# The first MLP product of one and a half batches, between the attention units, by seven block products

## The chip, the cores and the metric

The kernel runs on one core of a Trainium2 chip. A core has engines that work side by side, each with a queue of its own that it takes strictly in order: TensorE (PE: matmuls, with its weight loads shown as PEld), VectorE (DVE), ScalarE (ACT), GpSimd (POOL) and SyncE (SP), which here only issues DMAs. Matmul results go to PSUM, everything else lies in SBUF. The metric is the device time of one execution in microseconds (us). A difference under 0.5% counts as none.

## What is computed

One cross-attention block with its MLP, in fp32, for B = 4 batches of 512 rows of x and 512 rows of context, D = 512, 16 heads of 32, an inner width of 2048. Cut to what matters:

```python
h = layer_norm(x, ln1_w, ln1_b)
q = h @ q_w + q_b;  k = ctx @ k_w + k_b;  v = ctx @ v_w + v_b       # 16 heads of 32
attn = softmax(where(mask, q @ k.T / sqrt(32), -max))
hidden = (attn @ v) @ cproj_w + cproj_b + x
y = layer_norm(hidden, ln2_w, ln2_b)
y = gelu_tanh(y @ fc_w + fc_b)                                      # 512 -> 2048, "fc"
out = hidden + y @ proj_w + proj_b                                  # 2048 -> 512, "proj"
```

## The kernel before

**Units.** The attention is cut into NW = 16 groups `w` (batch w // 4, four heads each) times four tiles of 128 query rows: 64 units, u = 4w + qt. A unit issues `scores` (L252): PE puts the scores of four heads into `sc`, the one score buffer of four PSUM banks, so the scores of the next unit wait until the four minimum operations on VectorE (L263, output `ptt` and `mn`, with the mask `mb`) have read it; ACT takes four exps (L267). Then `turn` (L271) transposes the exps on VectorE into `tb` (L282); in odd units it also takes the reciprocal of the sums (L287), copies it on ACT (`rr`, L289) and transposes the rest (L290, L291). After two units, `exchange` (L300) sends `tb` to `pT` by 16 DMAs (L325), which SP's queue issues one by one. There is one `pT` for most pairs of units: the next exchange is issued only once `attend` (L328) of the pair before has multiplied its result into `oT` (VectorE, L347). `attend` is the matmuls `av` (L342); "attend 26" in the prediction is that of the 26th pair. Where a pair takes place is set by AT and LAG.

**Work between units.** PE's other work is put between the units by lists written out by hand: `first[w]` and `later[w]`, of chains such as `prep_k`, `prep_q`, `prep_v`, `cproj` (`accc`), the transposes of a norm (`tp`), fc (`accf`) and proj (`accp`). Where an entry is a tuple, its four members belong to the four units; otherwise `run` (L725) shares the list among the units by its costs, CHAIN = 3.4 and TURN = 0.5. `some(n)` takes the next n pieces of the MLP list: all fc and proj of batch 0, then those of half of batch 1 (SPLIT = 1, FIRST = 2 quarters). LN2 of a batch is `stat2`, `ln_rs` (`rs`, on GpSimd), `norm2` (L147) and `ln2_turn`, which leaves `yT`. GpSimd adds biases to the residual rows (`c_bias`, `proj_bias`, L354) and to v (L249).

**fc before.** `fc(b, f)` (L445) is four matmuls of 128 x 128 by 128 x 512 into one PSUM bank and one gelu by ACT, straight from PSUM. exp and gelu need different tables in ACT, so each turn from one to the other is an ACT_TABLE_LOAD. Weights go through a ring of MW = 8 slots: `load_mlp` (L434) issues the next load on SP's queue when the work that used a slot is issued.

**The tail.** What is left after the last unit, half of batch 1 and all of batches 2 and 3, is done in `last_mlps` (L513) with seven products of blocks in place of eight (Strassen's scheme in Winograd's form): for a pair of f, `fc_pair` (L541) forms sums of weight blocks (`a_sums`), sums of `yT`'s blocks (`b_sums`, in `y_sums`), seven products of two matmuls 128 x 128 by 128 x 256 each into four half-banks (`q`), and four adds on VectorE (L531) that put the results together, a copy of one on ACT (`p1`, L564) and four gelus. `project` does the same for proj (q1p to q7p).

Of the kernel before, what the change touches and what calls it, by code (L numbers as in the profile page):

```python
# [52 lines left out]
def xattn_block(ctx: ExitStack, tc: tile.TileContext, x, encT, mask, q_w, k_w, v_w, c_w, fc_w, p_w, vecs, rows, out):  # L53
# [391 lines left out]
    def fc(b, f):  # L445
        q, k = divmod(f, FQ)
        acc = acc_tile(f"accf_{b}_{f}")
        for d in range(ND):
            nc.tensor.matmul(acc, S["fcw", b, f][:, d, :], S["yT", b][:, d, :], start=(d == 0), stop=(d == ND - 1))  # L449
        nc.scalar.activation(  # L450
            gT[q % 2][:, k, :], acc, AF.Gelu_apprx_tanh, bias=vec[:, FCB + f : FCB + f + 1], scale=1.0
        )
# [22 lines left out]


    NP = NF // 2
    HL = L // 2

    def sub(o, x0, x1):  # L480
        nc.vector.tensor_tensor(o, x0, x1, ALU.subtract)  # L481

    def a_sums(a11, a12, a21, a22, s1, s2, s3, s4):
        nc.vector.tensor_tensor(s1, a21, a22, ALU.add)
        sub(s3, a11, a21)
        sub(s2, s1, a11)
        sub(s4, a12, s2)

    def b_sums(b11, b12, b21, b22, t1, t2, t3, t4):
        sub(t1, b12, b11)  # L490
        sub(t2, b22, t1)
        sub(t3, b22, b12)
        sub(t4, b21, t2)
# [19 lines left out]
    def last_mlps():  # L513
        last, ring = pools(ctx, last=1, ring=2)
        ps_last = ctx.enter_context(tc.tile_pool(name="ps_last", bufs=4, space=PSUM))
        ys = last.tile([P, 4, 2, HL], F32, tag="ys", name="ys")
# [10 lines left out]
        def acc_half(name):  # L527
            return acc_tile(name).rearrange("p (i l) -> p i l", i=2)

        def add(engine, o, x0, x1):  # L530
            engine.tensor_tensor(o, x0, x1, ALU.add)  # L531

        def y_blocks(b):
            return [S["yT", b][:, 2 * k : 2 * k + 2, j * HL : (j + 1) * HL] for k in range(2) for j in range(2)]

# [5 lines left out]
        def fc_pair(b, c, first, sums):  # L541
            a11, a12, a21, a22 = (wa[c % 2][:, i, 2 * k : 2 * k + 2] for i in range(2) for k in range(2))
            y11, y12, y21, y22 = y_blocks(b)
            s1, s2, s3, s4 = (ws[c % 2][:, i] for i in range(4))
# [4 lines left out]
            uc, u34, h = (ring.tile([P, 2, HL], F32, tag=n, name=f"{n}_{b}_{c}") for n in ("uc", "u34", "h"))

            def product(o, a, y):
                for k in range(2):
                    nc.tensor.matmul(o, a[:, k], y[:, k], start=(k == 0), stop=(k == 1))  # L553
# [391 lines left out]
```

## Time and profile before

| | us |
|---|---|
| median of 3 executions | 810.03 |
| lowest and highest | 807.67, 810.45 |
| profiled execution | 810.09 |
| its span, first to last instruction | 808.3 |
| PE busy, share | 791.9, 98% |
| DVE busy, share | 553.6, 68% |
| ACT busy, share | 360.8, 45% |
| POOL busy, share | 98.0, 12% |
| the tail's products begin at | 558.7 |

How to read the lines: a group's line has the source line, engine, operation, outputs and inputs by the program's names, shapes and the number of instructions; after the first bar the busy time and the mean time of one in nanoseconds; after the second the idle time of the engine just before them and what ended it. A timeline's line has the start, the duration, the engine, the line and the operation; idle time of the engine before it stands in brackets with its releaser. The chain of work goes back from the last instruction to what released each step; its lines have start, duration, what. A table by windows gives the stretch, its length, the busy time of PE, PEld, DVE, ACT and POOL with instructions in brackets, the share of full TensorE clock granted, the DMA share and GB/s.

### The profile page before, as it was taken

To read this page: it belongs to the slowest core of one execution; us is meant where nothing else is said; L and a number is where in the kernel's file an instruction comes from. 1 tells how busy PE (TensorE), PEld (TensorE's weight loads), DVE (VectorE), ACT (ScalarE), POOL (GpSimd) and SP (SyncE) were. 2 spreads that over 40 slices of the span, in tenths; PEclk is the share of its full clock that TensorE was granted. 3 is DMA by queue.
4 is the path that set the end of the run, shared out by engine and by line. 5 is a ranking of instruction groups with operands and counts; after the bars stand their busy time and mean duration, and the time that the engine had idled before them with its cause. 6 is when DMAs were issued, how large, how long until landed. Compare 5 with 4: busy or idle time off the path is not lost.

```text
span 808.3 us, 11790 instructions
## 1 busy us (share of the span) xinstructions
PE 791.9 (98%) x4082; PEld 481.2 (60%) x4082; DVE 553.6 (68%) x1145; ACT 360.8 (45%) x785; POOL 98.0 (12%) x112
## 2 busy tenths in 40 slices
PE   9999999979999999999999999999999999999998
PEld 6545455544454544535554333446888888888887
DVE  3788998876678665877778997636738993368511
ACT  2666755638673646556643469600312330023200
POOL 1110030030000030001131000120050021200011
PEclk9999999989999999999999999999999999999999
DMA  9889989837797877778768799883335330023001
GB/s 329 287 222 244 241 219 265 225 96 185 185 245 176 223 201 191 176 197 201 177 140 218 196 259 226 216 252 117 108 100 181 107 117 14 27 79 92 1 14 39
DMA packets 60955, 137.13 MB, mean 170 GB/s; under 512 B 12464, under 2 KB 15664, under 8 KB 60768
## 3 DMA queue, kind: packets, MB, share of 16 engines
q1 hardware_dynamic: 59472, 132.43, 61.2%
q0 software_dynamic: 896, 2.82, 1.1%
q10 hardware_dynamic: 528, 1.14, 0.7%
q8 instruction: 32, 0.52, 0.3%
q14 instruction: 27, 0.22, 0.1%
HBM read 58.22 MB, written 6.82 MB: 80 GB/s over the span
## 4 chain that ended last, share of the span: by engine, by line
PE 80%; DVE 7%; SPq 7%; DMA 3%; issue 1%; POOL 0%; ACT 0%; DVEq 0%; POOLq 0%
PE q L553 15%; PE accf L449 9%; PE accp L459 8%; PE accc L383 7%; SPq L325 7%; PE av L342 6%; PE sc L259 6%; PE acck L215 4%; PE accq L225 4%; PE accv L237 4%; DVE ptt L263 3%; PE q5p L593 2%; PE q3p L593 2%; PE q7p L593 2%; PE q6p L593 2%; PE q1p L593 2%
## 5 line engine op out<-in xcount | busy, mean ns | idle before, releaser
L267 ACT ACTIVATE ptt<-ptt,mn 128x512 f32<-128x512 f32 x256 | 182.2, 713 | 142.8 <-DVE mn L263 142.6
L263 DVE CUSTOM_DVE_ANT_0 ptt<-sc,mb 128x512 f32<-128x512 f32 x256 | 161.1, 685 | 45.6 <-PE sc L259 45.5
L282 DVE STREAM_TRANSPOSE tb<-ptt 128x1024 f32<-128x1024 f32 x96 | 119.1, 1242 | 10.4 <-ACT ptt L267 8.0
L449 PE MATMUL accf<-yT,pbt 128*128 128x512 f32 x192 | 87.3, 601 | 0.0
L459 PE MATMUL accp<-pbt,gt 128*128 128x512 f32 x192 | 86.5, 600 | 0.0
L259 PE MATMUL sc<-pbt 32*128 32x512 f32 x512 | 73.1, 640 | 4.8 <-DVE mn L263 2.6
L553 PE MATMUL q<-ys,gt 128*128 128x256 f32 x320 | 75.1, 379 | 0.0
L553 PEld LDWEIGHTS q<-ys,gt 128*128 128x128 f32 x320 | 60.8, 190 | 8.3
L449 PEld LDWEIGHTS accf<-yT,pbt 128*128 128x128 f32 x192 | 35.0, 190 | 50.2 <-issue 45.4
L459 PEld LDWEIGHTS accp<-pbt,gt 128*128 128x128 f32 x192 | 35.2, 190 | 48.8 <-issue 45.8
L237 PEld LDWEIGHTS accv<-ptt,xe 128*128 128x128 f32 x512 | 58.9, 192 | 8.2 <-issue 5.4
L237 PE MATMUL accv<-ptt,xe 128*128 128x128 f32 x512 | 60.5, 276 | 0.0
L215 PE MATMUL acck<-xe,ptt 128*128 128x512 f32 x128 | 59.0, 603 | 0.0
L553 PE MATMUL q<-yT,gt 128*128 128x256 f32 x240 | 58.1, 379 | 0.5 <-DVE gt L481 0.5
L225 PE MATMUL accq<-xe,ptt 128*128 128x512 f32 x128 | 58.4, 599 | 0.0
L383 PE MATMUL accc<-wc,oT 128*128 128x512 f32 x128 | 56.6, 596 | 0.0
L249 POOL TENSOR_TENSOR v<-v,row 128x512 f32<-128x512 f32 x16 | 20.4, 1274 | 278.5 <-ACT v L242 278.4
L557 ACT ACTIVATE ga<-uc,vec 128x256 f32<-128x256 f32 x40 | 20.4, 511 | 75.5 <-DVE uc L531 75.5
L553 PEld LDWEIGHTS q<-yT,gt 128*128 128x128 f32 x240 | 45.5, 190 | 7.4 <-DVE gt L481 0.9
L342 PE MATMUL av<-pT,v 128*32 128x256 f32 x768 | 48.1, 392 | 1.6 <-DMA pT<-tb 1.5
L267 ACT ACTIVATION_READ_ACCUMULATOR ptt<-ptt,mn 128x1 f32 x256 | 48.3, 189 | 0.0
L564 ACT COPY p<-q 128x256 f32<-128x256 f32 x20 | 7.1, 354 | 92.0 <-PE q L553 92.0
(121 smaller groups left out, 957.9 us busy)
## 6 DMA issues: line engine op xcount, KB each, us to landing
pT<-tb SPq DMA_DIRECT2D x384, 136.0 KB, 2.4
pbt<-p_w_dram SPq DMA_DIRECT2D x40, 256.0 KB, 3.1
gt<-fc_w_dram SPq DMA_DIRECT2D x40, 256.0 KB, 2.7
gt<-tb SPq DMA_DIRECT2D x64, 136.0 KB, 3.4
xe<-tb SPq DMA_DIRECT2D x56, 136.0 KB, 3.3
pbt<-fc_w_dram SPq DMA_DIRECT2D x24, 256.0 KB, 4.3
ptt<-k_w_dram SPq DMA_DIRECT2D x16, 256.0 KB, 3.9
xe<-encT_dram SPq DMA_DIRECT2D x16, 256.0 KB, 4.8
```

The source lines that it names most:

```text
L215: nc.tensor.matmul(acc, S["wk", w][:, d, :], eT[:, d, :], start=(d == 0), stop=(d == ND - 1))
L225: nc.tensor.matmul(acc, S["wq", w][:, d, :], xT[:, d, :], start=(d == 0), stop=(d == ND - 1))
L237: nc.tensor.matmul(acc[:, ts(t, P)], eT[:, d, ts(t, P)], S["wv", w][:, d, :], start=(d == 0), stop=(d == ND - 1),)
L259: nc.tensor.matmul(sc[:, h, :], qT[r, ts(qt, P)], kT[r, :], start=True, stop=True)
L263: nc.vector.tensor_tensor_reduce(out=s, in0=sc[:, h, :], in1=S["mb", w // NG], scale=1.0, scalar=FMAX, op0=ALU.add, op1=ALU.min, accum_out=mn,
L267: nc.scalar.activation(s, s, AF.Exp, bias=mn, scale=-1.0, accum_out=sums[:, qt, h : h + 1])
L282: nc.vector.transpose(*two_heads[k])
L342: nc.tensor.matmul(av[ts(h, HD), : 2 * P].rearrange(shape, **kw), v[:, t, ts(h, HD)], p[t][h], start=(t == 0), stop=(t == NT - 1),)
L383: nc.tensor.matmul(acc, S["oT", b][:, g, ts(t, P)], wc[:, g, :], start=(g == 0), stop=(g == NG - 1))
L449: nc.tensor.matmul(acc, S["fcw", b, f][:, d, :], S["yT", b][:, d, :], start=(d == 0), stop=(d == ND - 1))
L459: nc.tensor.matmul(acc, gT[q % 2][:, k, ts(t, P)], S["pw", b, q * FQ + k], start=(k == 0), stop=(k == FQ - 1))
L553: nc.tensor.matmul(o, a[:, k], y[:, k], start=(k == 0), stop=(k == 1))
```

## The change

The fc of batch 0 and of the first half of batch 1, done between the units, take the tail's scheme: `fc(b, c)` computes a pair of f by `fc_seven`, which the tail now calls too.

- Weights: three sums into `wsum` (two buffers) and one, s3, in place in the weight slot, by four adds of 128 x 256 on GpSimd for each pair; `fc_sums` issues them up to two pairs ahead, once the weights' loads have been issued.
- `yT`: three sums into `ys` and one, t3, in place in `yT`, four adds of 128 x 512 on VectorE for each batch (`y_sums`), in unit 21 for batch 0 and unit 47 for batch 1. For batch 1 they were at the start of the tail.
- Products: q1 and q26 lie in two `acc` banks, q57 and q34 in two more (in the tail: in two of its own half tiles); a copy of q1 on ACT (one buffer `p1`); four VectorE adds that write `gT` in place; then two gelus of 128 x 512 in place. In the tail the gelus were four of 128 x 256, each right after its add, and the first pair used s4 earlier.
- Order: a pair counts as two in `some(n)`; units with one fc now have a pair or none. Before, fc stood in units 22, 23, 25, 45, 58 (two each) and 26, 27, 31, 33, 36, 37, 42, 43, 57 and 59 to 63 (one each); now pairs stand in 22, 23, 25, 26, 33, 37, 42 and 45 (batch 0) and 57, 58, 60 and 62 (batch 1). Proj moves with it: some of batch 0's come later.
- `ys` and `wsum` are held from the start; the SBUF kept for GpSimd's DMA descriptors goes from its default to 4096 bytes.

```diff
@@ -87,6 +87,9 @@
     pb = pbt.rearrange("p (c i n) -> p c i n", c=NF // 2, i=2)
     pt = ptt.rearrange("p (s c n) -> p s c n", s=3, c=NF // 2)
 
+    ys = const.tile([P, 3, 2, L // 2], F32, tag="ys", name="ys")
+    wsum = const.tile([P, 2, 3, 2, P], F32, tag="wsum", name="wsum")
+
...
-    def fc(b, f):
-        q, k = divmod(f, FQ)
-        acc = acc_tile(f"accf_{b}_{f}")
-        for d in range(ND):
-            nc.tensor.matmul(acc, S["fcw", b, f][:, d, :], S["yT", b][:, d, :], start=(d == 0), stop=(d == ND - 1))
-        nc.scalar.activation(
-            gT[q % 2][:, k, :], acc, AF.Gelu_apprx_tanh, bias=vec[:, FCB + f : FCB + f + 1], scale=1.0
-        )
-        count[1] += 1
+    def a_sums(a11, a12, a21, a22, s1, s2, s3, s4, engine=None):
+        add(engine or nc.vector, s1, a21, a22)
+        sub(s3, a11, a21, engine)
+        sub(s2, s1, a11, engine)
+        sub(s4, a12, s2, engine)
+    def b_sums(b11, b12, b21, b22, t1, t2, t3, t4):
+        sub(t1, b12, b11)
+        sub(t2, b22, t1)
+        sub(t3, b22, b12)
+        sub(t4, b21, t2)
+    def y_blocks(b):
+        return [S["yT", b][:, 2 * k : 2 * k + 2, j * HL : (j + 1) * HL] for k in range(2) for j in range(2)]
+    def y_sums(b):
+        y = y_blocks(b)
+        b_sums(*y, ys[:, 0], ys[:, 1], y[1], ys[:, 2])
+    def fc_seven(b, c, g, a, s, half):
+        y11, t3, y21, y22 = y_blocks(b)
+        t1, t2, t4 = (ys[:, i] for i in range(3))
+        s1, s2, s3, s4 = s
+        q1, q26 = (acc_half(f"{n}_{b}_{c}") for n in ("q1", "q26"))
+        q57, q34 = (half(f"{n}_{b}_{c}") for n in ("q57", "q34"))
+        p1 = small.tile([P, HL], F32, tag="p1", bufs=1, name=f"p1_{b}_{c}")
+        g = g.rearrange("p i (j l) -> p (i j) l", j=2)
+        def product(o, x, y):
+            for k in range(2):
+                nc.tensor.matmul(o, x[:, k], y[:, k], start=(k == 0), stop=(k == 1))
+        product(q1[:, 0], a[0][:, 0:2], y11)
+        nc.scalar.copy(p1, q1[:, 0])
+        product(q26[:, 0], a[0][:, 2:4], y21)
+        product(q26[:, 1], s2, t2)
+        add(nc.vector, g[:, 0:4:3], q26, p1[:, None, :].broadcast_to([P, 2, HL]))
+        product(q57[:, 1], s3, t3)
+        product(q57[:, 0], s1, t1)
+        u2 = g[:, 3:4]
+        add(nc.vector, g[:, 1:3], q57, u2.broadcast_to([P, 2, HL]))
+        add(nc.vector, g[:, 3], q57[:, 0], g[:, 2])
+        product(q34[:, 0], s4, y22)
+        product(q34[:, 1], a[1][:, 2:4], t4)
+        add(nc.vector, g[:, 1:3], q34, g[:, 1:3])
+        for i in range(2):
+            f = 2 * c + i
+            h = g[:, 2 * i : 2 * i + 2]
+            nc.scalar.activation(h, h, AF.Gelu_apprx_tanh, bias=vec[:, FCB + f : FCB + f + 1], scale=1.0)
+    fc_pairs = [(b, q * FQ // 2 + i) for b in range(SPLIT + 1) for q in range(NQ if b < SPLIT else FIRST) for i in range(2)]
+    def raw_pair(b, c):
+        return [S["fcw", b, 2 * c + i] for i in range(2)]
+    def fc_sums():
+        while count[3] < len(fc_pairs) and count[3] < count[4] + 2:
+            b, c = fc_pairs[count[3]]
+            if ("fcw", b, 2 * c + 1) not in S:
+                return
+            x, y = raw_pair(b, c)
+            s = wsum[:, count[3] % 2]
+            a_sums(x[:, :2], x[:, 2:], y[:, :2], y[:, 2:], s[:, 0], s[:, 1], y[:, :2], s[:, 2], nc.gpsimd)
+            S["ws", b, c] = s[:, 0], s[:, 1], y[:, :2], s[:, 2]
+            count[3] += 1
+    def fc(b, c):
+        q, k = divmod(2 * c, FQ)
+        fc_seven(b, c, gT[q % 2][:, k : k + 2, :], raw_pair(b, c), S["ws", b, c], acc_half)
+        count[1] += 2
+        count[4] += 1
         load_mlp()
+        fc_sums()
 
...
-        def fc_pair(b, c, first, sums):
-            a11, a12, a21, a22 = (wa[c % 2][:, i, 2 * k : 2 * k + 2] for i in range(2) for k in range(2))
-            y11, y12, y21, y22 = y_blocks(b)
-            s1, s2, s3, s4 = (ws[c % 2][:, i] for i in range(4))
-            t1, t2, t3, t4 = (ys[:, i] for i in range(4))
-            q1, q62 = (acc_half(f"{n}_{b}_{c}") for n in ("q1", "q62"))
-            q75, q43 = (half_tile(f"{n}_{b}_{c}") for n in ("q75", "q43"))
-            p1 = ring.tile([P, HL], F32, tag="p1", name=f"p1_{b}_{c}")
-            uc, u34, h = (ring.tile([P, 2, HL], F32, tag=n, name=f"{n}_{b}_{c}") for n in ("uc", "u34", "h"))
-            def product(o, a, y):
-                for k in range(2):
-                    nc.tensor.matmul(o, a[:, k], y[:, k], start=(k == 0), stop=(k == 1))
-            def gelu(i, j, src):
-                f = 2 * c + i
-                nc.scalar.activation(
-                    ga[:, c, i, j * HL : (j + 1) * HL], src, AF.Gelu_apprx_tanh,
-                    bias=vec[:, FCB + f : FCB + f + 1], scale=1.0,
-                )
+        def fc_pair(b, c, sums):
             sums()
-            product(q1[:, 0], a11, y11)
-            nc.scalar.copy(p1, q1[:, 0])
-            product(q62[:, 1], a12, y21)
-            if first:
-                product(q43[:, 1], s4, y22)
-            product(q62[:, 0], s2, t2)
-            add(nc.vector, uc, q62, p1[:, None, :].broadcast_to([P, 2, HL]))
-            gelu(0, 0, uc[:, 1])
-            product(q75[:, 0], s3, t3)
-            product(q75[:, 1], s1, t1)
-            add(nc.vector, u34, q75, uc[:, :1].broadcast_to([P, 2, HL]))
-            add(nc.vector, uc[:, 0], q75[:, 1], u34[:, 0])
-            gelu(1, 1, uc[:, 0])
-            if not first:
-                product(q43[:, 1], s4, y22)
-            product(q43[:, 0], a22, t4)
-            add(nc.vector, h, q43, u34)
-            gelu(1, 0, h[:, 0])
-            gelu(0, 1, h[:, 1])
+            fc_seven(b, c, ga[:, c], [wa[c % 2][:, i] for i in range(2)],
+                     [ws[c % 2][:, i] for i in range(4)], half_tile)
...
-        y_sums(SPLIT)
...
-        return [(CHAIN, lambda f=f: fc(b, f)) for f in range(q * FQ, (q + 1) * FQ)]
+        return [(2 * CHAIN * 7 / 8, lambda c=c: fc(b, c)) for c in range(q * FQ // 2, (q + 1) * FQ // 2)]
...
-        taken, mlp[:n] = mlp[:n], []
+        taken = []
+        while n > 0:
+            n -= 1 if mlp[0][0] == CHAIN else 2
+            taken.append(mlp.pop(0))
+        assert n == 0
...
-    first[4] = x1 + [k, q, v] + x4
+    first[4] = x1 + [k, q, v] + x4 + do(fc_sums)
-        [k] + stat(0, 0, 1, 2, 3) + rs(0) + x3 + norm(0, 0, 1, 2, 3) + [v], [q] + t2, some(2) + pb_(0), some(2)
+        [k] + stat(0, 0, 1, 2, 3) + rs(0) + x3 + norm(0, 0, 1, 2, 3) + [v], [q] + t2 + do(lambda: y_sums(0)), some(2) + pb_(0), some(2)
-    first[7] = [k, q] + x2[:1] + some(2) + x2[1:2] + some(3) + [v]
+    first[7] = [k, q] + x2[:1] + some(2) + x2[1:2] + some(2) + [v]
-    first[8] = h_(1, 0, 1) + x2[2:] + [k, q] + x3[:2] + some(1) + x3[2:3] + [v] + x3[3:] + h_(1, 2, 3) + x4
+    first[8] = h_(1, 0, 1) + x2[2:] + [k, q] + x3[:2] + some(2) + x3[2:3] + [v] + x3[3:] + h_(1, 2, 3) + x4
...
-        t2[2:] + pb_(1) + some(1) + h_(2, 2, 3, 0, 1)
+        t2[2:] + do(lambda: y_sums(1)) + pb_(1) + some(1) + h_(2, 2, 3, 0, 1)
-    first[14] = some(1) + norm(2, 0, 1), some(1) + norm(2, 2, 3), some(2), some(1)
-    first[15] = hid_(1, 2, 3) + some(1), some(1), some(1), some(2)
+    first[14] = some(1) + norm(2, 0, 1), norm(2, 2, 3) + some(2), some(2), []
+    first[15] = hid_(1, 2, 3) + some(2), [], some(2), some(1)
...
-    nc = bacc.Bacc("TRN2", target_bir_lowering=False, num_devices=1)
+    nc = bacc.Bacc("TRN2", target_bir_lowering=False, num_devices=1, dynamic_dma_scratch_size=4096)
```

More of the change, by code (lines that the diff above doesn't have):

```diff
@@ L113, in xattn_block @@
     S = {}
-    count = [0, 0, 0]
+    count = [0, 0, 0, 0, 0]
     Q = [nc.sync]
@@ L443, in load_mlp, with sub @@
             count[0] += 1
-    def fc(b, f):
-        q, k = divmod(f, FQ)
-        acc = acc_tile(f"accf_{b}_{f}")
-        for d in range(ND):
-            nc.tensor.matmul(acc, S["fcw", b, f][:, d, :], S["yT", b][:, d, :], start=(d == 0), stop=(d == ND - 1))
-        nc.scalar.activation(
-            gT[q % 2][:, k, :], acc, AF.Gelu_apprx_tanh, bias=vec[:, FCB + f : FCB + f + 1], scale=1.0
-        )
-        count[1] += 1
+    NP = NF // 2
+    HL = L // 2
+    def sub(o, x0, x1, engine=None):
+        (engine or nc.vector).tensor_tensor(o, x0, x1, ALU.subtract)
@@ new lines, in add @@
+    def add(engine, o, x0, x1):
+        engine.tensor_tensor(o, x0, x1, ALU.add)
+    def a_sums(a11, a12, a21, a22, s1, s2, s3, s4, engine=None):
[10 more added lines that the diff above has]
+        return [S["yT", b][:, 2 * k : 2 * k + 2, j * HL : (j + 1) * HL] for k in range(2) for j in range(2)]
@@ new lines, in y_sums, with acc_half @@
+    def y_sums(b):
+        y = y_blocks(b)
+        b_sums(*y, ys[:, 0], ys[:, 1], y[1], ys[:, 2])
+    def acc_half(name):
+        return acc_tile(name).rearrange("p (i l) -> p i l", i=2)
+    def fc_seven(b, c, g, a, s, half):
[26 more added lines that the diff above has]
+            nc.scalar.activation(h, h, AF.Gelu_apprx_tanh, bias=vec[:, FCB + f : FCB + f + 1], scale=1.0)
@@ L467, in proj @@
         load_mlp()
[L477 to L493, printed above, removed]
+        fc_sums()
     wa = [gt[:, i * 2048 : i * 2048 + 1024].rearrange("p (i d f) -> p i d f", i=2, d=ND) for i in range(2)]
@@ L513, in last_mlps @@
     def last_mlps():
-        last, ring = pools(ctx, last=1, ring=2)
+        last, = pools(ctx, last=1)
         ps_last = ctx.enter_context(tc.tile_pool(name="ps_last", bufs=4, space=PSUM))
-        ys = last.tile([P, 4, 2, HL], F32, tag="ys", name="ys")
         ga = last.tile([P, NP, 2, L], F32, tag="ga", name="ga")
@@ L525, in half_tile @@
             return ps_last.tile([P, 2, HL], F32, tag="half", name=name)
[L527 to L534, printed above, removed]
         def g_sums(c):
@@ L639, in project @@
                 nc.sync.dma_start(out=out[b, ts(2 + t, P), :HL], in_=hid(1, 0, t))
-        def y_sums(b):
-            b_sums(*y_blocks(b), *(ys[:, i] for i in range(4)))
-        y_sums(SPLIT)
         half = FIRST * FQ // 2
@@ L653, in last_mlps @@
                         nc.sync.dma_start(out=pb[:, c, i, :], in_=p_w[ts(2 * c + i, P), :])
-                fc_pair(b, c, c == pairs[0], lambda: sum_wa(c + 1) if c + 1 < NP else None)
+                fc_pair(b, c, lambda: sum_wa(c + 1) if c + 1 < NP else None)
                 if c + 2 < NP:
```

## The prediction

> **What bounds the kernel now.** I read the share of busy time, then the costliest groups, then the chain of work that ended last, and after that the timeline around every place where a removed or added instruction stands. TensorE is the bound: it is busy for all but some 16 us.
>
> ```profile
> PE   791.9 (98%) x4082; PEld 481.2 (60%) x4082; DVE 553.6 (68%) x1145; ACT 360.8 (45%) x785; POOL 98.0 (12%) x112
> PE 80%; DVE 7%; SPq 7%; DMA 3%; issue 1%; POOL 0%; ACT 0%; DVEq 0%; POOLq 0%
> ```
>
> So work taken from PE is worth its time, as long as the order around it doesn't begin to wait. The change trades PE time for time on VectorE, ScalarE and GpSimd; whether these have it to spare depends on the place.
>
> **1. The products (batch 0: −6.7; batch 1: −3.6 if nothing waits).** Removed are 24 fc of four matmuls, added 12 pairs of 14 matmuls of half the width. The groups give both prices, since the tail already works with such products:
>
> ```profile
> L449 PE MATMUL accf<-yT,pbt 128*128 128x512 f32 x192 | 87.3, 601 | 0.0
> L553 PE MATMUL q<-ys,gt 128*128 128x256 f32 x320 | 75.1, 379 | 0.0
> ```
>
> A record is half a matmul and their times overlap, so I take the pitch: an fc alone takes 3.43 to 3.63 us on the timeline, and the 24 together 85.4 (batch 0's 16: 56.6; batch 1's eight: 28.75, 0.94 of it idle). In the chain, the tail's first 112 records, four pairs, take 24.17 us: 6.04 a pair, and I allow 0.2 to change over (a lone fc's 3.63 against 3.43).
>
> ```profile
> 558.66 24.17 PE q L553 x112
> ```
>
> Twelve pairs: 74.9. Gain 10.3, of it 6.7 in batch 0 and 3.6 in batch 1.
>
> A pair adds four VectorE adds (pitch 0.61 + 0.61 + 0.34 + 0.61 = 2.2 us, from the tail's 692 and 425 ns groups less overlap) and a copy on ACT (354 ns); its two gelus no longer read PSUM and cost what they did (688 ns). For batch 0 (units 22 to 45) VectorE is busy 59.3 of 85.75 and 61.0 of 89.17 us there, so 18 us of adds find room under PE. Moved PE work changes the exchanges: 16 issues on SP's queue (10.0 to 11.4 us) plus landing must fit between two attends. Attends 26 to 28 get 12.1 us of PE work against 12.65 to 13.9 needed: +0.8; two other intervals have 12.8 to 12.9: +0.2; and a wait of 0.98 for an exchange near 369 gets 15.5 us of cover: −1.0. Together 0, bounds −1 and +2. The 48 weight sums on GpSimd (724 ns each by the nearest row) lie under its 12%.
>
> **2. Units 20 to 22 (−2.9).** Today four row adds on GpSimd meet the four norms of LN2 on VectorE. A norm takes 531 to 541 ns in its other groups; here four take 4.86 us, PE then waits, and its clock halves (granted 0.51 from 171.9 to 178.8, 1.00 before and after):
>
> ```profile
> 164.13 4.86 DVE L147 TENSOR_SCALAR xn<-h,mv,rs 128x512 f32<-128x512 f32 x4 [1.40 <-POOL rs L133]
> 165.80 5.56 POOL L354 TENSOR_TENSOR h<-h,row 128x512 f32<-128x512 f32 x4 [0.36 <-DVE xn L147]
> 173.89 1.11 PE L156 MATMUL tp<-ident,xn 128*128 128x128 f32 x4 [3.64 <-ACT pbt L228]
> 174.93 3.64 PE L342 MATMUL av<-pT,v 128*32 128x256 f32 x32
> ```
>
> In the new order these row adds stand on GpSimd's queue behind the weight sums of the third pair, whose buffer is free only after the first pair's products, near 182. The norms run free: −1.65 at least. If the clock then doesn't drop, the slow stretch (an attend of 3.64 where others take 1.86, the turns 0.5 more) is saved too: 2.4. I take half of that: −2.9, bounds −1.7 and −4. The four output sums of batch 0 in unit 21 delay one exchange by 2 us that has slack.
>
> **3. The output sums of batch 1 (+6.3, and +1.5 for the clock).** They go into unit 47, ahead of `h`, `mb` and of the oT that lets the next exchange begin. Today (VectorE, then GpSimd, then the chain):
>
> ```profile
> 405.61 0.68 DVE L463 TENSOR_TENSOR h<-accp,h 128x512 f32<-128x512 f32 x1
> 406.98 0.41 DVE L347 TENSOR_TENSOR oT<-av,pT 128x256 f32<-128x256 f32 x1
> ```
> ```profile
> 405.51 1.27 POOL L354 TENSOR_TENSOR h<-h,row 128x512 f32<-128x512 f32 x1 [2.49 <-DMA h<-x_dram]
> 407.15 3.73 POOL L354 TENSOR_TENSOR h<-h,row 128x512 f32<-128x512 f32 x3 [0.37 <-DVE mb L195]
> ```
> ```profile
> 416.86 2.38 DMA pT<-tb
> 419.37 1.93 PE av L342 x32
> ```
>
> The exchange fills the time from oT to the attend; there is no slack, so what delays oT delays PE. Clean, four sums cost 2.4 us (684 and 688 ns, overlapping). But both inputs lie in SBUF, and four GpSimd row adds run just then. In the tail the same meeting is seen, VectorE first, GpSimd below:
>
> ```profile
> 661.82 1.78 DVE L481 TENSOR_TENSOR gs<-ga,gs 128x512 f32<-128x512 f32 x1
> 664.23 1.64 DVE L481 TENSOR_TENSOR ptt<-pbt,ptt 128x512 f32<-128x512 f32 x1
> ```
> ```profile
> 661.78 1.27 POOL L354 TENSOR_TENSOR hid<-hid,row 128x512 f32<-128x512 f32 x1 [24.34 <-DMA hid<-xa]
> 663.67 5.00 POOL L354 TENSOR_TENSOR hid<-hid,row 128x512 f32<-128x512 f32 x3 [0.63 <-DMA hid<-xa]
> ```
>
> Such an add takes 1.64 to 1.78 in place of 0.69. Four of them, at about 1.6, make oT and the attend of unit 50 late by 6.3 (bounds 2.4 and 6.5). PE then stands idle longer than the 3.64 us that halved its clock in part 2: 0 to 2.4 more, I take 1.5. Term: +7.8, bounds +2.4 and +8.9.
>
> **4. Units 57 to 63 (+5.75 in place of −3.6, and +1.7 for the clock).** Here PE was about level with a loop over ACT and VectorE. ACT per unit: four exps, table load, gelu, table load back:
>
> ```profile
> 477.52 1.28 ACT L450 ACT_TABLE_LOAD   x1
> 478.82 0.69 ACT L450 ACTIVATE gt<-accf,vec 128x512 f32<-128x512 f32 x1
> 479.53 1.28 ACT L267 ACT_TABLE_LOAD   x1
> 480.82 0.72 ACT L267 ACTIVATE ptt<-ptt,mn 128x512 f32<-128x512 f32 x1
> ```
> ```profile
> 470.04:512.89 42.85, 41.91 (x220) 16.77 (x217) 36.34 (x80) 37.92 (x72) 3.27 (x3) 1.00 0.93 246
> ```
>
> The second line's columns are PE, PEld, DVE, ACT, GpSimd: ACT is busy 37.9 of 42.85. A gelu waited for PE alone; now it waits for adds, which stand behind the transposes on VectorE's queue, which wait for the exps; and the next exps wait for the gelus and the load. One loop of a unit with a pair: exps 2.86, end of the exps to the end of the transposes 1.3 (even unit) or 1.68 (odd, with reciprocal), adds 2.2, gelus 1.27, load 1.28, steps 0.05: 8.96 or 9.34. A unit without a pair: 2.86 + 1.68 + 0.69 (first min) = 5.23. The pairs stand in 57, 58, 60 and 62, so from the exps of 57 to those of 63 it takes 9.34 + 8.96 + 5.23 + 8.96 + 5.23 + 8.96 = 46.7, where today it is 514.06 − 473.89 = 40.2. The scores of a unit need the mins of the one before (one score buffer), and units 59 and 61 hold no other PE work: PE waits some 6 us before the scores of 60 and 4 before those of 62. Carried through these steps, sc(63) ends 5.1 later than today. Ahead of it, the norms of batch 2 wait for `rs` on GpSimd, behind eight weight sums (724 ns each; their weights land near 465): +0.65, bounds 0 and 2. Sum +5.75. Bounds: −3.6, if adds and gelus slip into gaps, and +7. The clock can fall in either gap: 0 to 4.4, I take 1.7.
>
> **Weighed against the Trainium skill.** "TensorE: Matmul & The Clock Gate", What's actually happening, says that the clock halves after a whole idle window of about 3.4 us in a window that runs freely; by that a 4 us gap would seldom trip it and a 6 us gap mostly would, and the clock's terms would be some 1 us smaller. The row of 3.64 us above did trip it. "ScalarE: Activation LUTs", What ACT_TABLE_LOAD costs, has 2.66 us for a switch, a drain of 1380 ns included. Here gelu starts 1.30 after its load starts, so this trace doesn't show the drain; by the page each loop with a pair would be 1.4 us longer and the sum about 5 us more.
>
> **5. The tail (+0.3, bounds −0.3 and +0.8).** PE bounds it at 6.04 a pair before and after; the output sums leave its start, where other PE work hides them. The first projection waits for gelus of 512 that start later, 0.5; the sum s4 is no longer wanted first, −0.2. The smaller reserve of SBUF for GpSimd's descriptors shows in no row of before: taken as 0.
>
> **Sum.** −6.7 + 0 − 2.9 + 7.8 + 5.75 + 1.7 + 0.3 = +6.0 (rounded). The profiled execution took 810.1 (span 808.3 and 1.8 around it), the median is 810.0: **816**.
>
> **Rivals.**
> - *Faster: the loop of units 57 to 63 doesn't bind.* For: VectorE is idle 6.5 of 42.85 us there. It decides where the adds come ahead of the transposes' wait. Then part 4 gives −3.6 and no clock: 816 − 11.05 = 805. Against: the queues are in order, and the adds stand behind the transposes.
> - *Same: the output sums of batch 1 run clean*, since the rows from `h<-x_dram` land a few us earlier or later. Part 3 is 2.4: 810.6. Against: 407.15 shows three rows in one go.
> - *Both*: 799.6.
> - *Slower still: the clock halves at all three gaps*, and SP's exchanges, now started late, miss further attends: +0.9 + 2.7 + 1.5 = 821.
> - *The change doesn't do what it says*: the order of PE shows 12 pairs in place of 24 fc, so this is out.
>
> **How the numbers follow.** As summed 0.46 (own range 812 to 819); sums clean 0.22; loop hidden 0.10; both 0.05; slower still 0.17. 0.5% is 4 us, about what a measurement here can tell: faster is below 806, slower above 814. Slower: 0.85 of the first, 0.1 of the second, all of the last: 0.58. Faster: most of the loop's case, both, and some of the second: 0.15. Same 0.27. Range for 8 in 10: 804.5 to 821.
>
> **What would show it.** Right: attend 50 waits over 3 us for pT; VectorE adds of 1.6 us in unit 47; PE idle before the scores of 60 and 62 with "DVE mn" as releaser; norms of 0.5 us near 165; PE's busy time down by some 10 us. Wrong: adds of 0.69 in unit 47; scores 60 and 62 not waiting; the first proj after unit 63 less than 3 us later against the scores of 57 than today's 42.85; exchanges late in batch 0.

## The result, and the profile after

The changed kernel takes 818.2 us (median of four executions, 815.6 to 821.0), the kernel before 810.2 in the same session: 1.011 times as long, 95% interval 1.006 to 1.015. It is slower, by 8 us; 816 was forecast. The profiled execution took 821.0 with a span of 819.3 and is the longest of the four, so the trace shows some 3 us more than the median.

The page of the changed kernel, first the shares of the engines, then the chain by engine:

```profile
PE 790.1 (96%) x4226; PEld 512.9 (63%) x4226; DVE 586.2 (72%) x1197; ACT 335.1 (41%) x745; POOL 134.4 (16%) x160
PE 79%; DVE 8%; SPq 6%; ACT 2%; DMA 2%; issue 2%; POOL 1%; DVEq 0%; POOLq 0%; ACTq 0%
```

PE's busy time fell by 1.8 us only, although some 10 us of products are gone. Parts of what is left ran at half clock: in the profile, 20.5 us of the span between units 21 and 62 (before: 6.8, in units 21 and 22). What PE waited for, by cause (total, number, longest):

```profile
PE sc L262 <- DVE mn L266: 7.6, 4, 2.7
PE av L345 <- DMA pT<-tb: 6.0, 3, 4.6
PE av L345 <- ACT p L494: 3.2, 2, 2.5
```

Before, the first two were 2.6 and 1.5 and the third did not exist. ACT is less busy than before (335 in place of 361 us, mostly by 26 table loads in place of 38, 15 us, and by 40 gelus of 512 columns in the tail in place of 80 of 256, 12 us), and yet new waits end at ACT. To find the places, I set the start of the scores and attends of each unit side by side in the two traces and read off how far the changed kernel was ahead (-) or behind (+):

| at | start before | start after | difference | step |
|---|---|---|---|---|
| scores of unit 21 | 163.40 | 164.88 | +1.5 | +1.5 |
| scores of unit 22 | 178.50 | 177.22 | -1.3 | -2.8 |
| scores of unit 48 | 405.84 | 399.45 | -6.4 | -5.1 |
| scores of unit 50 | 421.24 | 420.90 | -0.3 | +6.1 |
| first proj after unit 63 | 512.89 | 524.01 | +11.1 | +11.5 |
| end of PE's work | 805.05 | 816.05 | +11.0 | -0.1 |

The first step, ahead of anything the change touches on PE, differs between executions: the scores of unit 0 alone begin at 21.5 to 22.9 in the traces of this study, and from there to the scores of unit 21 it takes 140.5 to 143.7. So a step of one trace is good to about 1 us at best; where several traces share an order, their range is given below.

**Unit 47.** VectorE's timeline, then GpSimd's, then PE's at the attend:

```profile
398.52 0.77 DVE L162 TENSOR_SCALAR yT<-tp,vec 128x512 f32<-128x512 f32 x1
399.21 0.68 DVE L452 TENSOR_TENSOR ys<-yT 128x512 f32<-128x512 f32 x1
400.00 0.69 DVE L452 TENSOR_TENSOR ys<-yT,ys 128x512 f32<-128x512 f32 x1
400.60 1.76 DVE L452 TENSOR_TENSOR yT<-yT 128x512 f32<-128x512 f32 x1
402.28 1.75 DVE L452 TENSOR_TENSOR ys<-yT,ys 128x512 f32<-128x512 f32 x1
403.96 0.68 DVE L543 TENSOR_TENSOR h<-accp,h 128x512 f32<-128x512 f32 x1
404.56 0.88 DVE L198 TENSOR_SCALAR mb<-m 128x512 f32<-128x512 uint8 x1
405.36 0.41 DVE L350 TENSOR_TENSOR oT<-av,pT 128x256 f32<-128x256 f32 x1
```
```profile
400.04 6.53 POOL L357 TENSOR_TENSOR h<-h,row 128x512 f32<-128x512 f32 x4 [3.43 <-DVE ys L452]
```
```profile
417.73 3.23 PE L345 MATMUL av<-pT,v 128*32 128x256 f32 x32 [4.56 <-DMA pT<-tb]
```

From yT to oT 6.84 us pass, where it was 2.06; the wait for pT is 4.56, where it was 0.48. Two of the four sums, not all, meet the row adds and take 1.76. The attend then takes 3.23 in place of 1.93, at half clock. The meeting slows both sides: the four row adds take 1.5 to 1.8 each, 1.3 where nothing meets them.

**Units 57 to 63.** One pass of the new loop, unit 58 (ACT, then VectorE), and PE's line that waits for it:

```profile
485.74 0.72 ACT L270 ACTIVATE ptt<-ptt,mn 128x512 f32<-128x512 f32 x1
...
488.57 0.35 ACT L494 COPY p<-q 128x256 f32<-128x256 f32 x1
488.94 1.28 ACT L509 ACT_TABLE_LOAD   x1
492.60 1.33 ACT L509 ACTIVATE gt<-gt,vec 128x512 f32<-128x512 f32 x2 [2.38 <-DVE gt L455]
493.95 1.28 ACT L270 ACT_TABLE_LOAD   x1
495.25 0.72 ACT L270 ACTIVATE ptt<-ptt,mn 128x512 f32<-128x512 f32 x1
```
```profile
488.70 1.25 DVE L285 STREAM_TRANSPOSE tb<-ptt 128x1024 f32<-128x1024 f32 x1 [0.17 <-ACT ptt L270]
489.87 0.65 DVE L455 TENSOR_TENSOR gt<-q,p 128x512 f32<-128x512 f32 x1
490.62 1.95 DVE L455 TENSOR_TENSOR gt<-q,gt 128x512 f32<-128x512 f32 x3
```
```profile
488.98 3.45 PE L345 MATMUL av<-xe,v 128*32 128x256 f32 x32 [2.47 <-ACT p L494]
496.15 2.09 PE L262 MATMUL sc<-pbt 32*128 32x512 f32 x8 [2.66 <-DVE mn L266]
```

Exps, transposes, adds, gelus, table load, exps: 485.74 to 495.25 is 9.51, forecast as 8.96. The copy p1 (`p<-q`) stands behind the exps on ACT's queue, and attend 27 waits for the PSUM bank that it empties. The chain of work that ends in the first proj after unit 63 goes through this wait: the exps of 58 up to 488.67, the copy, attend 27, the scores and minimum operations of 59, the scores of 60.

### The profile page after: what moved, and what is told of

Read it like the earlier page. It is cut to its first block, busy times and chain, and to the rows that moved or that the text cites. A ratio compares the mean times of both kernels' runs of the same rounds, so it can differ in the third digit from the quotient of the medians.

```text
span 819.3 us, 12241 instructions
## 1 busy us (share of the span) xinstructions
PE 790.1 (96%) x4226; PEld 512.9 (63%) x4226; DVE 586.2 (72%) x1197; ACT 335.1 (41%) x745; POOL 134.4 (16%) x160
## 4 chain that ended last, share of the span: by engine, by line
PE 79%; DVE 8%; SPq 6%; ACT 2%; DMA 2%; issue 2%; POOL 1%; DVEq 0%; POOLq 0%; ACTq 0%
PE q L491 20%; PE accp L539 10%; PE sc L262 7%; PE av L345 6%; PE accv L240 5%; PE acck L218 5%; SPq L328 5%; PE accc L386 5%; PE accq L228 4%; DVE ptt L266 3%; PE q4p L607 2%; PE q3p L607 2%; PE q7p L607 2%; PE q2p L607 2%; PE q5p L607 2%; PE q6p L607 2%
## 5 line engine op out<-in xcount | busy, mean ns | idle before, releaser
L285 DVE STREAM_TRANSPOSE tb<-ptt 128x1024 f32<-128x1024 f32 x96 | 119.1, 1242 | 14.2 <-ACT ptt L270 10.3
L262 PE MATMUL sc<-pbt 32*128 32x512 f32 x512 | 74.9, 655 | 9.7 <-DVE mn L266 7.6
L491 PE MATMUL q<-yT,gt 128*128 128x256 f32 x320 | 78.9, 379 | 0.0
L491 PEld LDWEIGHTS q<-yT,gt 128*128 128x128 f32 x320 | 60.8, 190 | 8.7 <-issue 0.5
L509 ACT ACTIVATE ga<-ga,vec 128x512 f32<-128x512 f32 x40 | 26.7, 715 | 85.6 <-DVE ga L455 85.6
L491 PE MATMUL q<-ys,gt 128*128 128x256 f32 x240 | 61.7, 379 | 0.0
L494 ACT COPY p<-q 128x256 f32<-128x256 f32 x32 | 11.4, 355 | 94.8 <-PE q L491 94.8
L491 PEld LDWEIGHTS q<-ys,gt 128*128 128x128 f32 x240 | 45.5, 190 | 6.6 <-DVE gt L452 0.4
L262 PEld LDWEIGHTS sc<-pbt 32*128 32x128 f32 x512 | 20.4, 186 | 42.8 <-issue 19.2
L345 PEld LDWEIGHTS av<-pT,v 128*32 128x32 f32 x768 | 24.4, 113 | 33.1 <-issue 17.0
```

Of the source, the lines that this page charges most:

```text
L262: nc.tensor.matmul(sc[:, h, :], qT[r, ts(qt, P)], kT[r, :], start=True, stop=True)
L285: nc.vector.transpose(*two_heads[k])
L345: nc.tensor.matmul(av[ts(h, HD), : 2 * P].rearrange(shape, **kw), v[:, t, ts(h, HD)], p[t][h], start=(t == 0), stop=(t == NT - 1),)
L491: nc.tensor.matmul(o, x[:, k], y[:, k], start=(k == 0), stop=(k == 1))
```

## The experiments

Times are medians; the ratio is to the kernel before, run on the same chip beside it, with its 95% interval. Where the intervals of two kernels overlap, their times do not tell them apart; what is at one place is then read from the traces.

| kernel | median us | ratio |
|---|---|---|
| changed kernel | 818.2 | 1.011 (1.006 to 1.015) |
| batch 0 alone | 803.1 | 0.991 (0.989 to 0.993) |
| output sums later | 812.9 | 1.003 (1.001 to 1.004) |
| row adds later | 818.6 | 1.010 (1.008 to 1.012) |
| dummy matmuls | 817.5 | 1.009 (1.006 to 1.011) |
| no table loads | 820.6 | 1.013 (1.011 to 1.014) |
| pairs spread, proj between | 828.9 | 1.023 (1.021 to 1.025) |
| the same, output sums later | 820.8 | 1.013 (1.012 to 1.015) |
| kernel before, row adds of unit 22 later | 807.1 | 0.996 (0.995 to 0.998) |
| first product and copy ahead | 816.6 | 1.007 (1.004 to 1.010) |
| batch 0 alone, the same | 802.4 | 0.990 (0.988 to 0.992) |
| pairs two units apart | 818.7 | 1.010 (1.007 to 1.014) |

### Batch 0 alone

```diff
-    fc_pairs = [(b, q * FQ // 2 + i) for b in range(SPLIT + 1) for q in range(NQ if b < SPLIT else FIRST) for i in range(2)]
+    fc_pairs = [(b, q * FQ // 2 + i) for b in range(SPLIT) for q in range(NQ) for i in range(2)]
...
+        if b == SPLIT:
+            return [(CHAIN, lambda f=f: fc_old(b, f)) for f in range(q * FQ, (q + 1) * FQ)]
...
-        t2[2:] + do(lambda: y_sums(1)) + pb_(1) + some(1) + h_(2, 2, 3, 0, 1)
+        t2[2:] + pb_(1) + some(1) + h_(2, 2, 3, 0, 1)
```

`fc_old` is fc as it was; `first[14]` and `first[15]` are those of before, and `y_sums(SPLIT)` stands at the start of the tail again.

> Batch 0 keeps the seven products; batch 1's eight fc are four matmuls again, in their old units, and its output sums stand at the start of the tail again. Theory A (two places lose the time: the output sums in unit 47, about 6 us, and units 57 to 63, about 11 us of which 6 are the clock; batch 0 and units 20 to 22 gain 5 and 3): 802, range 800 to 805. Rival B (the loss is spread: 33 us more on VectorE and 36 us more on GpSimd slow everything a little, batch 0's two thirds of it included): 812 to 816, slower than before.

Measured 803.1, 7.1 less than before. Theory A holds; theory B would have kept two thirds of the loss. PE's waits on this kernel are about those of before (in unit 21 2.5 in place of 3.6), with one new one over 0.5 us:

```profile
PE av L345 <- ACT p L494: 1.6, 1, 1.6
```

### Output sums of batch 1 later

```diff
-        t2[2:] + do(lambda: y_sums(1)) + pb_(1) + some(1) + h_(2, 2, 3, 0, 1)
+        t2[2:] + pb_(1) + some(1) + h_(2, 2, 3, 0, 1)
-    first[12] = [k, q], cb(2) + [v], c[:2], c[2:]
+    first[12] = [k, q], cb(2) + [v], c[:2], c[2:] + do(lambda: y_sums(1))
```

> Only the four output sums of batch 1 move, from unit 47 (ahead of the oT that starts an exchange) to the end of unit 51. Theory A: the 4.6 us wait of attend 23 and the half clock behind it go, 6 us less than the changed kernel: 812, range 810 to 814. Rival B (spread load): as the changed kernel, 818.

Measured 812.9, 5.3 less than the changed kernel. The same four sums cost nothing that can be told where no exchange waits behind them: the attend of unit 50 now reads

```profile
412.35 1.93 PE L345 MATMUL av<-pT,v 128*32 128x256 f32 x32 [0.31 <-DMA pT<-tb]
```

Against batch 0 alone this kernel has the pairs of batch 1 as its addition, and the output sums of batch 1 in unit 51 in place of the start of the tail: 812.9 - 803.1 = 9.8 us is what these pairs lose, in place of the 3.6 that their products were to save.

### Row adds later

```diff
-        t2[2:] + do(lambda: y_sums(1)) + pb_(1) + some(1) + h_(2, 2, 3, 0, 1)
+        t2[2:] + do(lambda: y_sums(1)) + pb_(1) + some(1)
-    first[12] = [k, q], cb(2) + [v], c[:2], c[2:]
+    first[12] = [k, q] + h_(2, 2, 3, 0, 1), cb(2) + [v], c[:2], c[2:]
```

> Output sums stay in unit 47; the loads of the four residual rows, whose row adds on GpSimd met the sums, are issued one unit later. If the meeting with GpSimd is what made two of the sums 1.76 in place of 0.69 us: all four take 0.69, oT comes 2.1 us earlier, 816, or 814.5 if the shorter gap keeps the clock up. If the sums' own 2.5 us are the whole matter, or the sums are slow for another reason: 818, two sums still at 1.7.

```profile
399.45 0.68 DVE L452 TENSOR_TENSOR yT<-yT 128x512 f32<-128x512 f32 x1
400.06 0.69 DVE L452 TENSOR_TENSOR ys<-yT,ys 128x512 f32<-128x512 f32 x1
...
401.59 0.42 DVE L350 TENSOR_TENSOR oT<-av,pT 128x256 f32<-128x256 f32 x1
```
```profile
414.23 3.54 PE L345 MATMUL av<-pT,v 128*32 128x256 f32 x32 [2.88 <-DMA pT<-tb]
```

With the row adds out of the way the two slow sums take 0.68 and 0.69, oT follows yT by 4.22 us in place of 6.84, and the wait falls from 4.56 to 2.88. So the meeting of the engines is shown, by the trace. The time, 818.6, does not show these 2 us. What stays is the sums' own length in that place: a wait of 2.88 where it was 0.48, and the clock halved all the same (the attend took 3.54).

### Dummy matmuls in the empty units

```diff
+    def dummy():
+        acc = acc_tile(f"dummy_{count[0]}_{len(mlp)}")
+        for _ in range(9):
+            nc.tensor.matmul(acc[:, :P], ident, ident, start=True, stop=True)
+    first[14] = *first[14][:3], do(dummy)
+    first[15] = first[15][0], do(dummy), *first[15][2:]
```

> The changed kernel with nine small matmuls whose result nobody reads in each of the empty units 59 and 61, 2.5 us of PE that only keeps it busy. If the half clock in units 58 to 63 costs time of its own: windows at half clock from 492 on go and the time falls by 3 to 5 us, to 814. If the loop over ACT and VectorE sets the pace there and the slow clock hides under it: 817 to 819.

No stretch of half clock is left after 489, and yet the time is 817.5, within the uncertainty of no change. From the exps of 57 to those of 63 it still takes 49.8 (changed kernel: 50.1). In the trace 2.2 us are won between the scores of 57 and the first proj after 63 (52.1 in place of 54.3). The loop sets the pace, and most of the matmuls that ran slowly ran under it. So the half clock after 489 costs some 2 us there, and not the 6 that theory A of the first experiment had put down to the clock; the stretch before 489, with attend 27 at 3.42, stayed as it was.

### No table loads

```diff
-            nc.scalar.activation(h, h, AF.Gelu_apprx_tanh, bias=vec[:, FCB + f : FCB + f + 1], scale=1.0)
+            nc.scalar.activation(h, h, AF.Exp if b == SPLIT and c < FIRST * FQ // 2 else AF.Gelu_apprx_tanh, bias=vec[:, FCB + f : FCB + f + 1], scale=1.0)
```

> In the units, the eight gelus of batch 1 are replaced by exps of the same shape and place, so ACT loads no table between units 57 and 63 (the output is not the reference's). If the loop exps, transposes, adds, gelus, table load, exps sets the pace in units 57 to 63: each of the four loops with a pair loses the load back of 1.28, 4 to 5 us in all, 813. Rival (the wait for a PSUM bank behind the copy p1, or the adds alone, set it): under 1.5 us, 817.

```profile
482.09 1.33 ACT L509 ACTIVATE gt<-gt,vec 128x512 f32<-128x512 f32 x2 [4.30 <-DVE gt L455]
483.33 0.70 ACT L270 ACTIVATE ptt<-ptt,mn 128x512 f32<-128x512 f32 x1
...
490.18 1.33 ACT L509 ACTIVATE gt<-gt,vec 128x512 f32<-128x512 f32 x2 [3.68 <-DVE gt L455]
491.42 0.71 ACT L270 ACTIVATE ptt<-ptt,mn 128x512 f32<-128x512 f32 x1
```

The loops of 57 and 58 became 1.42 shorter each (9.41 and 8.09, where the changed kernel has 10.83 and 9.51), that of 60 longer (10.29 for 9.79; its scores fell into a stretch of half clock), and 57 to 63 took 47.6 for 50.1. So the load back is on the path of a loop, as expected, but the loops gave 2.5 us and not 4 to 5, and the whole kernel took 820.6, where 813 was expected. Relative to unit 57 it was 2.0 ahead at the scores of 63 and gave 3.3 back before attend 30. There the last of the 16 issues of an exchange on SP's queue stands at 531.2, the one before it at 520.4. It signals by the semaphore that a load of proj weights, issued at 508.7, had used; whether the queue was held for that was not tried. The experiment says what a loop costs, but not what the kernel would take.

### The pairs spread, with proj pieces between them

```diff
-    mlp += FC(SPLIT, 0) + FC(SPLIT, 1) + PJ(SPLIT, 0) + PJ(SPLIT, 1)
+    f, g, p, r = FC(SPLIT, 0), FC(SPLIT, 1), PJ(SPLIT, 0), mlp.pop()
+    mlp += f[:1] + [r] + f[1:] + p[:2] + g[:1] + p[2:] + g[1:] + PJ(SPLIT, 1)
...
-    first[14] = some(1) + norm(2, 0, 1), norm(2, 2, 3) + some(2), some(2), []
-    first[15] = hid_(1, 2, 3) + some(2), [], some(2), some(1)
+    first[14] = some(2) + norm(2, 0, 1), norm(2, 2, 3) + some(1), some(2), some(1)
+    first[15] = hid_(1, 2, 3) + some(1), some(2), some(2), some(2)
```

The ring loads the weights of `PJ(SPLIT, 0)` ahead of those of `FC(SPLIT, 1)`. The second run has the output sums at the end of unit 51 besides.

> The same work, but the four pairs of batch 1 stand in units 56, 58, 61 and 63, and proj pieces stand in every unit between them. Theory A: PE has work while the loop over ACT and VectorE runs, its waits in units 57 to 63 fall from 9.6 us to under 3 and the clock stays up: 10 us less than the changed kernel, 808, range 805 to 811. Rival (the loop of 9 us per pair delays the scores wherever it stands): 814 to 818.

> Both moves: pairs of batch 1 spread as in the run before, and its output sums at the end of unit 51. Theory A: the two losses add, 16 us less than the changed kernel: 802, range 799 to 805, faster than the kernel before by 1%. Rival B (spread load): over 810.

Both missed: 828.9 and 820.8. The proj pieces that were to fill PE waited for their own weights:

```profile
496.95 6.22 PE L543 MATMUL accp<-pbt,gt 128*128 128x512 f32 x8 [5.99 <-DMA pbt<-p_w_dram]
544.61 1.19 PE L543 MATMUL accp<-pbt,gt 128*128 128x512 f32 x1 [8.53 <-DMA pbt<-p_w_dram]
```

The loads can be issued only when a slot of the ring of eight is free, and then stand behind 16 issues of an exchange (10 to 11 us) on SP's queue. This says nothing on the loop; it says that the ring and SP's queue leave no proj to put there. The two runs differ by 8.1 us through the output sums alone, more than the 5.3 above.

### The kernel before, with the row adds of unit 22 later

```diff
-        [k] + stat(0, 0, 1, 2, 3) + rs(0) + x3 + norm(0, 0, 1, 2, 3) + [v], [q] + t2, some(2) + pb_(0), some(2)
+        [k] + stat(0, 0, 1, 2, 3) + rs(0) + x3 + norm(0, 0, 1, 2, 3) + [v], [q] + t2, some(2), some(2)
-    first[6] = [k, q] + some(4) + [v] + x1
+    first[6] = [k, q] + some(4) + [v] + pb_(0) + x1
```

> The kernel before, with one edit: the four row adds of proj_bias(0) are queued on GpSimd behind the bias of v of unit 24 and so no longer meet the norms of LN2. If that meeting is what the change wins by in units 20 to 22: 2.8 us less, 807.3 (bounds 806 and 808.4). Rival (the new order wins there by something else): 810.

```profile
166.31 2.98 DVE L147 TENSOR_SCALAR xn<-h,mv,rs 128x512 f32<-128x512 f32 x4 [1.40 <-POOL rs L133]
```
```profile
174.17 0.66 PE L156 MATMUL tp<-ident,xn 128*128 128x128 f32 x4 [2.49 <-ACT pbt L228]
174.84 1.93 PE L342 MATMUL av<-pT,v 128*32 128x256 f32 x32
```

Measured 807.1, 3.1 less than before: four norms take 2.98 us instead of 4.86, PE's wait is 2.49 instead of 3.64, the clock stays up (attend 1.93). One moved line of the old kernel brings what the change won there, and it is part of batch 0 alone as well. The shorter wait alone doesn't explain that the clock stayed up: PE waits the same 2.49 in the changed kernel, where the clock did fall (the last section shows why).

### The first product and its copy ahead of the scores

```diff
+            if u in (23, 58, 60, 62):
+                q1_ahead()
             scores(w, qt)
             turn(w, qt)
```

`q1_ahead` issues `product(q1)` and the copy p1 of the unit's pair. With batch 0 alone it is done in unit 23 only.

> The changed kernel; the first product of the pairs in units 23, 58, 60 and 62, and the ACT copy p1 that empties its PSUM bank, are issued ahead of the unit's scores and exps instead of behind them. If attends 10 and 27 waited (0.71 and 2.47 us) for a bank whose copy stood behind exps in ACT's queue, both waits go: 3 us less in these two places, 1 to 3 in the whole, since the loop over ACT and VectorE behind attend 27 stays: 815 to 817. Rival (the waits have another cause, or the loop takes all of it back): attend 27 still waits, 818.

> Batch 0 alone by seven products, and the pair of unit 23 with its first product and copy ahead of the scores. Attend 10 waited 1.57 us for that bank in the run with batch 0 alone: 801.6 where that run had 803.1 (range 800.5 to 803). Rival (the exchange is due at that time anyway): 803.

```profile
486.47 1.93 PE L345 MATMUL av<-xe,v 128*32 128x256 f32 x32
488.33 1.14 PE L262 MATMUL sc<-pbt 32*128 32x512 f32 x8
489.40 1.13 PE L483 MATMUL q<-yT,pbt 128*128 128x256 f32 x4
494.21 2.01 PE L262 MATMUL sc<-pbt 32*128 32x512 f32 x8 [3.67 <-DVE mn L266]
```

Attends 10 and 27 wait no longer, so the banks were the cause. The kernel takes 816.6, as forecast, though its interval overlaps with that of the changed kernel. The scores of 60 wait 3.67 instead of 2.66 and come 26.4 after those of 57 in both kernels, and the exps of 57 to 63 take 50.1 as before: up to the scores of 60 the loop takes it all back. After them PE gains, though: from the scores of 57 to the first proj after 63 it takes 51.1 in place of 54.3, and the tail gives nothing back. In this part the trace has two steps of half clock in place of four, and the first products of 60 and 62 are done before their scores wait; the two were not taken apart. With batch 0 alone 802.4 was measured where 803.1 stood; the wait of 1.6 is gone from the trace, the time can't tell the two apart.

### The pairs two units apart

```diff
-    mlp += FC(SPLIT, 0) + FC(SPLIT, 1) + PJ(SPLIT, 0) + PJ(SPLIT, 1)
+    f, r = FC(SPLIT, 0), mlp.pop()
+    mlp += f[:1] + [r] + f[1:] + FC(SPLIT, 1) + PJ(SPLIT, 0) + PJ(SPLIT, 1)
...
-    first[13] = some(1), some(1) + stat(2, 0, 1), some(1) + stat(2, 2, 3) + rs(2), some(2)
-    first[14] = some(1) + norm(2, 0, 1), norm(2, 2, 3) + some(2), some(2), []
+    first[13] = some(2), some(1) + stat(2, 0, 1), some(1) + stat(2, 2, 3) + rs(2), some(1)
+    first[14] = some(2) + norm(2, 0, 1), norm(2, 2, 3) + some(1), some(2), []
```

> The changed kernel with the pairs of batch 1 in units 56, 58, 60 and 62 and the last proj piece of batch 0 in unit 57, no two pairs in neighbouring units, the weights' loads in their old order; PE has less left between the last scores and the tail by no piece. If units 57 to 63 are paced by one pass of the loop per pair (8.96 in an even unit, 9.34 in an odd one, 5.23 without a pair): from the exps of 57 to those of 63 42.6 in place of 46.7, and 3 to 5 us less in all: 814.5. Rival (PE's waits there come from the total of work on ACT and VectorE, wherever it stands): 817 to 819.

From the exps of 57 to those of 63 it took 46.0, 4.1 less, the difference that was expected. The time is that of the rival: 818.7. Units 52 to 56 took back what 57 to 63 gave: from the exps of 52 to those of 63 85.9 in the changed kernel and 86.1 here (74.6 before). The new loss is at the unit where the first pair now stands:

```profile
464.62 1.94 PE L262 MATMUL sc<-pbt 32*128 32x512 f32 x8 [2.50 <-DVE mn L266]
```

Units 52 to 63 hold the last exps, LN2's work for batch 2 and the pairs; moving a pair among them moves the wait.

The times from exps to exps, by unit, read from ACT's timeline:

| from the exps of | 56 | 57 | 58 | 59 | 60 | 61 | 62 | 57 to 63 |
|---|---|---|---|---|---|---|---|---|
| before | 6.68 | 6.93 | 6.87 | 6.93 | 6.25 | 6.93 | 6.25 | 40.2 |
| changed kernel | 8.05 | 10.83 | 9.51 | 5.23 | 9.79 | 5.23 | 9.52 | 50.1 |
| dummy matmuls | 8.47 | 10.82 | 9.52 | 5.23 | 9.52 | 5.23 | 9.52 | 49.8 |
| no table loads | 8.42 | 9.41 | 8.09 | 5.21 | 10.29 | 5.23 | 9.39 | 47.6 |
| pairs two units apart | 9.51 | 6.73 | 9.51 | 5.23 | 9.81 | 5.22 | 9.51 | 46.0 |

## Why the prediction was right

816 was forecast, 818.2 measured, in the range and slower as said. By its steps, against the profiled execution:

| step | forecast | measured |
|---|---|---|
| 1 batch 0: products and exchanges | -6.7 | -5.1 |
| 2 units 20 to 22 | -2.9 | -2.8 |
| 3 output sums of batch 1, clock included | +7.8 | +6.1 |
| 4 units 57 to 63, clock included | +7.45 | +11.5 |
| 5 tail | +0.3 | -0.1 |

The steps add up to +9.6 in this trace, to +6.0 in the forecast; the medians differ by 8.0. Batch 0 and units 57 to 63 came out 1.6 and 4.0 worse than forecast, the output sums 1.7 better: that the total fits better than its terms is in part luck. One slip of the working: 85.4 - 74.9 is 10.5, not 10.3, so batch 1's products were worth 3.8 and not 3.6; only the faster rival uses it.

- *Batch 0.* The gain is there. The waits at the exchanges and banks were set off to 0. They were 0.71, 0.42, 0.44 and 0.28 (1.85) against the 0.98 that went, so +0.9. The 0.71 (1.57 with batch 0 alone) is a wait that I did not name: a PSUM bank behind the copy p1. In the nine traces with this wait the step is -3.8 to -5.9; in the two with the first product ahead in unit 23, which don't have it, it is -6.7 and -6.9, the forecast. So the products gain what was summed, and the miss goes with the wait; what it takes along beside its own 0.7 to 1.6 us was not traced.
- *Units 20 to 22.* Right in mechanism, and shown by the one line moved in the kernel before. Not all four norms had met the row adds: the last two did (1.5 us each), and the first takes 1.6 in either kernel, beside the bias of v on GpSimd. Here the clock did drop, for 3.4 us instead of 6.8; with batch 0 alone it did not. Over all traces without the meeting the step is -2.4 to -3.1 where the clock drops (six of them) and -4.0 where it doesn't (six), which is the prediction's bound for a clock that stays up. The -2.9 was a figure half-way; that it meets this trace's -2.8 is in part luck. The norms of the changed kernel, 2.97 us in place of 4.86:

```profile
165.59 2.97 DVE L150 TENSOR_SCALAR xn<-h,mv,rs 128x512 f32<-128x512 f32 x4 [1.41 <-POOL rs L136]
```

- *Output sums.* Right in place and kind. "Four of them, at about 1.6" was wrong: two meet GpSimd's adds, two don't, since GpSimd's first row add itself waited until 400.04. The sums with what follows made oT 4.8 late after yT rather than 6.3, and the clock took 1.3 at the attend.
- *Units 57 to 63.* The loop was right, down to the 5.23 of a unit without a pair. Its terms were too small: the adds take 2.70 (489.87 to 492.57) where 2.2 had been worked out from the tail's groups with an overlap; here they don't overlap: each begins 0.03 to 0.10 after the end of the one before. Most likely it is because each of them reads, or writes over, what the one just before it wrote or read; that was not tried, but the output sums of "row adds later" look the same: the second, which reads the first, begins 0.78 after it, the third and the fourth, which don't read the one just before, 0.61. In the tail of the kernel before, two adds of a pair in such a row stand 0.73 apart as well (614.92 and 615.65), so the longer steps were there to be read. And two norms in unit 57, 0.96 together, were left out of its loop (9.34 + 0.5 + 0.96 = 10.8, measured 10.83). Together 50.1 - 46.7 = 3.4 us of the 4.0 missed, counted from exps to exps; the first proj doesn't wait for the exps of 63, and after the scores of 60 PE itself was slow, so the division is not exact. The clock, 1.7 in the sum, is worth 2.2 by the dummy matmuls' trace. PE's waits did not stand where the prediction had them: 2.66 each before the scores of 60 and 62 in place of 6 and 4, the rest before the products of 58 (0.68 and 1.08) and attend 27 (2.47).
- *The wait behind the copy* at attend 27 (2.47) is a mechanism that the prediction did not have. With it gone the loop kept the same pace, so the wait itself cost little; the 3.2 us that this kernel gained after the scores of 60 are not explained in full.
- *Tail.* No difference.
- *The rivals.* That the sums run clean was half right, since two of four did; but even all four clean left a wait of 2.88, and the step from the scores of 48 to those of 50 was +4.0 then, clock included, where that rival had 2.4. That the loop does not bind was wrong. Of the slower rival one half came true: the clock halved at all three gaps. The other half, further attends that miss their exchange, did not. That everything slows a little was not a rival in the prediction; batch 0 alone excludes it.

Why the median is under the sum of the trace is not settled: the executions differ by up to 5.5 us, and the profiled one was the longest. Not tried was a version that gives the pairs of batch 1 PE work that is ready, which would need other slots for the weights; so whether the 3.6 us can be had there stays open. The best kernels here do batch 0 alone by seven products (803.1 and 802.4) and beat both.

## What to carry to other kernels

A saving on the bound engine is worth its time only where the new operand chain fits into the slack of the engines that it passes; the same change won 7 us in a stretch with slack (3 of them by moving other work apart) and lost 15 in two without. Price the new chain as a loop, from one use to the next, with every instruction that its queues hold, and adds in a row by their full durations. Before putting cheap work ahead of an instruction, look at what that instruction lets begin: 2.6 us of sums ahead of an exchange cost 4.0 in the trace, with the clock, and 4.8 us of them, where they met GpSimd, 6.1.
